# Batch-1 loads and statistics moved, and two layernorms without GpSimd, in a four-layer kernel built around a selective scan

## The chip, the cores and the metric

One core of one Trainium2 chip runs the whole program as a single launch. The metric is the device time of that launch in microseconds. The engines are named as in the profile: PE is TensorE (matrix products and transposes), DVE is VectorE, ACT is ScalarE, POOL is GpSimd, SP is SyncE, which here only issues DMAs.

## The reference

`x` is (2, 512, 512) in float32. Four residual sub-layers follow one another:

```
x = x + ln(scan_layer(ln(x)))     # selective scan, 1024 channels, 16 states
x = x + ln(ffn_4bit(ln(x)))       # 512 -> 1376 -> 512, 4-bit weights, output rounded to float16
x = x + ln(attention(ln(x)))      # 32 query heads, one key and value head
x = x + ln(experts(ln(x)))        # shared expert, latent expert, scaled by top-2 logits

def scan_layer(h):                # h is (2, 512, 512)
    x, gate = split(h @ W_in.T)                       # 1024 channels each
    x = silu(conv_b + causal_conv4(x))
    ts, Bm, Cm = split(x @ W_x.T, [32, 16, 16])       # the "ranks"
    ts, Bm, Cm = rms(ts), rms(Bm), rms(Cm)
    dt = softplus(ts @ W_dt.T + b_dt)
    for t in range(512):
        state = state * exp(dt[t] * A) + (dt[t] * x[t]) * Bm[t]   # 1024 x 16
        y[t] = sum over the 16 states of state * Cm[t]
    y = (y + x * D) * silu(gate)
    return y @ W_out.T

def ln(x): return (x - mean(x)) / sqrt(var(x) + 1e-5)  # the last one also has a scale and a shift
```

The 4-bit weights are `q * s - (z + 1) * s` in groups of 128 rows. The feed-forward layer computes `(g * sigmoid(g) * u) @ Wd` with `g = h @ Wg` and `u = h @ Wu`.

## The kernel before

The rows of `x` are eight tiles of 128 x 512, four to a batch; `xs(b)` gives those of batch b. Within the scan layer the data is transposed: 128 channels on the partitions and 512 time steps along the row. The 1024 channels are eight blocks c, so two batches make 16 blocks k = 8b + c. The 16 states are handled two at a time, in eight groups gi. A "scan step" s is one pair (k, gi): there are 128.

**Phase 1, the head** (to about 64 us). Batch 0 is normalized, projected and convolved, the ranks of batch 0 are computed, and 4-bit words of the gate and up weights are unpacked and stored to DRAM (`wgu_d`). `ranks_norm` and `ranks_out` scale the ranks and store B and C to DRAM (`scr`), from which `states(b, gi, "B")` loads each pair of rows to all partitions. At the end SP issues the 16 B and C loads (B of group gi + 1 ahead of C of group gi), and then, by `issue_after(last.ins)`, the four loads of batch 1's `x`. The statistics of batch 1 need these.

**Phase 2, the scan phase** (to about 584 us). One scan step is spread over the engines:

- ACT: `exps(s + 2)`, the decay exp(dt A) into one of two PSUM tiles `da`.
- DVE: `times_B` (L1055), `bx = du * B` with `du` in PSUM, then `scan` (L1059), the recurrence along the row in place in `bx`.
- POOL: `times_C` (L1065), and for some steps an addition of the two states (L1067).
- PE: `sums` (L1087), which adds the states up in the PSUM tile `py` with an identity matrix. `ps_y` has one buffer, so the sums of block k + 1 begin after `fin(k)` (L1093), where DVE multiplies the sum by the gate.

`bx` has six buffers. Beside its sums PE works through a generator, `stream()`: the gates of batch 0, batch 1's normalized and transposed x (`turned("n1")`), its projections and ranks, the gates of batch 1, the output projection of batch 0 (`out_tiles`), the transposes of the next sub-layer's input (`turned("f0")`), and the gate and up projections of feed-forward 0 for batch 0 (`ffn0`, L984). The loop gives it a budget: a step is worth `STEP = 3.5` us and a matmul costs `MM = 0.86`. What the other engines do with a result is a job: a generator that `spawn(gen, lag)` enters and that `tick()` advances, two ticks to a scan step. The order in which this loop emits instructions is the order in which each engine executes them: `pin()` fixes it. Two PSUM banks serve the stream (`bank`, `release`). `pool_turn()` lets one such job a step use POOL.

Three parts of this phase matter here:

- `norm_job(1, "n1")` computes the mean and variance of batch 1's four x tiles on DVE (L798, L799), and normalizes them. It is spawned with a lag of 12 ticks.
- `ranks_norm(1)` and `ranks_out(1)` do for batch 1 what the head did for batch 0. L513 and L514 turn the sums of squares into means, and L542 copies B and C out of PSUM.
- `out_job(i, ps)` takes the output projection of tile i of batch 0, normalizes it (`add_normed`: statistics on DVE, the power -1/2 and the product with the mean on POOL, the scaling on ACT, the residual addition L892 on POOL), and then normalizes the sum for feed-forward 0 (`norm_one`). `st["f0", i]` is the tick from which `turned("f0")` may transpose it.

**Phase 3** (from about 584 us). PE does the output projection of batch 1 (L1176). Meanwhile `once(dq)` unpacks the 4-bit down weights into DRAM (`wd_d`): `zeros` on DVE after the last `fin`, a store and a load of the zeros `z_d` (SP), eight words on DVE (L326) and POOL (L327), and stores. The second projection of feed-forward 0 (`fo`, L1198) reads them back. Feed-forward for batch 1, attention and the experts follow.

`w4` tiles (weights on the SP queue) and the output weights `wo` share a pool of three buffers, so a load waits in SP's order until a buffer has been read.

Of the kernel before, what the change touches and what calls it, by code (L numbers as in the profile page):

```python
# [9 lines left out]
F32 = mybir.dt.float32  # L10
# [8 lines left out]
P = 128  # L19
# [37 lines left out]
def tile_sandwich(  # L57
# [50 lines left out]

    def w4(src, name, chunks=KH, cols=PW):
        t_ = wst.tile([P, KH, PW], F32, tag="w4", name=name)  # L110
        nc.sync.dma_start(out=t_[:, :chunks, :cols], in_=src)
        return t_
# [17 lines left out]
    def minus_mean(mv, rs, name, n=TB, beside_scan=False):  # L130
# [12 lines left out]
        return nm  # L143

# [281 lines left out]
    with ExitStack() as mamba:  # L426
# [75 lines left out]
        def ranks_norm(b, ps):  # L502
# [10 lines left out]
            nc.vector.tensor_scalar(r[:, :, 0], ss[:, :, 0], 1.0 / R_DT, 1e-6, ALU.mult, ALU.add)  # L513
            nc.vector.tensor_scalar(r[:, :, 1:], ss[:, :, 1:], 1.0 / N_ST, 1e-6, ALU.mult, ALU.add)  # L514
# [24 lines left out]
        def ranks_out(b, pt):  # L539
            bc = st["bc"] = jrow(f"bc{b}")  # L540
            nc.scalar.copy(dtT[b][:R_DT, :], pt[:R_DT])
            nc.vector.tensor_copy(bc[R_B:N_ROW], pt[R_B:N_ROW])  # L542
# [30 lines left out]
        with ExitStack() as p1:  # L573
# [76 lines left out]
            half_gate = mbank("pg0_1")  # L650
            for k in range(KH // 2):
                nc.tensor.matmul(
                    half_gate, w_in(1, 0, 0)[:, k, P : 2 * P], xT[0][:, k, :], start=(k == 0), stop=False
                )
            for _ in ranks_norm(0, pr):
                pass
            ranks_out(0, ranks_rows(0, bank1(0, "pt0")))

            for gi in range(NGI):
                if gi + 1 < NGI:  # L660
                    states(0, gi + 1, "B")
                states(0, gi, "C")
# [3 lines left out]
            with tc.issue_after(last.ins):  # L666
                load_x(1)
# [7 lines left out]
        with ExitStack() as p2:  # L675
# [75 lines left out]
            def gate(b, c):  # L751
# [3 lines left out]
                if (b, c) == (0, 1):  # L755
                    turns.append([f"pg{b}_{c}", None])
                    ps = half_gate
                    yield from in_proj(b, ps, w, c % 2, KH // 2)
# [34 lines left out]
            def norm_job(b, name):  # L793

                mv = stat.tile([P, TB, 2], F32, tag="mv", name=f"mv_{name}")
                for i, src in enumerate(xs(b)):
                    s6 = stat.tile([P, 6], F32, tag="st", name=f"st_{name}_{i}")
                    nc.vector.bn_stats(s6, src)  # L798
                    nc.vector.bn_aggr(mv[:, i, :], s6)  # L799
                    yield 1  # L800
                yield 1
                rs = rstd(mv, name)
                nm = minus_mean(mv, rs, name, TB, True)
# [10 lines left out]
            def turned(name, dst):  # L814

                for i in range(TB):
                    yield from until((name, i), 2)
# [11 lines left out]
                    spawn(out(), 2)  # L829
# [38 lines left out]
            def norm_one(b, i, name):  # L868

                mv = moments([xs(b)[i]], f"{name}_{i}")  # L870
                rs = rstd(mv, f"{name}_{i}", 1)
                nm = minus_mean(mv, rs, f"{name}_{i}", 1, True)
                yield 4
# [6 lines left out]
                st[name, i, "xn"] = xn  # L880

# [19 lines left out]

            def out_job(i, ps):
                o = jrow(f"o0_{i}")
                if i < TB - 1:
# [575 lines left out]
```

## Time and profile before

| | |
|---|---|
| median of 3 runs | 957.5 us (957.22 to 958.73) |
| the profiled execution | 955.66 us, of which the span is 953.7 us |
| mean granted PE clock | 0.965 |
| scan phase, scan 0_0 to the last sum | about 64 to 578 us |
| one scan step on DVE | 1.20 (L1055) + 2.28 (L1059) us, less an overlap |
| batch 1's x: the four loads issued | from 81.90 us |
| first and last statistics of batch 1 (L798, L799) | 91.53 to 100.35 us |
| output projection of batch 1 | from 583.31 us |
| second projection of feed-forward 0 | from 612.77 us |

The profile page was taken on one execution. Its slices cut the span into 40 parts of 23.8 us, and each digit is a busy share in tenths. A row of the timeline gives the start and the duration in us, the engine, the line, the operation, what it writes and reads, the shape, and in brackets the idle time before it with what ended it. Line numbers in the prediction are those of the kernel before.

### The profile page before, as it was taken

The page shows a single profiled execution, that of the slowest core. Times are in us where ns is not written, and L with a number is a line of the kernel's source. Part 1 is how long each engine was busy: PE and PEld are TensorE (multiplying, and loading weights), DVE is VectorE, ACT ScalarE, POOL GpSimd, SP SyncE. Part 2 cuts the span into 40 slices and gives each one's busy share as a digit, 9 for nine tenths or more (in the row PEclk, how much of TensorE's full clock was granted, in tenths as well). Part 3 has the DMA queues.
Part 4 walks back from the last instruction along what each step waited for, and adds up shares of the span by engine and source line. Part 5 has one row for each costly group of instructions (what it writes and reads, how often), then busy time and mean ns, then how long its engine had stood idle before and what let it go on. Part 6 is the DMA issues. An engine that isn't in the chain of part 4 may idle for free.

```text
span 953.7 us, 7163 instructions
## 1 busy us (share of the span) xinstructions
PE 860.8 (90%) x2188; PEld 385.4 (40%) x2188; DVE 672.4 (71%) x780; ACT 424.1 (44%) x638; POOL 486.8 (51%) x356
## 2 busy tenths in 40 slices
PE   6989778789999889589999999999999998999994
PEld 3433333334533434134434444444544444455441
DVE  5877999999999998999999995535600024525225
ACT  4356675656666655476655640125320013412122
POOL 7746796677877787876877884440000000011002
PEclk9989999888999999889999999999999999999998
DMA  6449111010002854200111103445222231100101
GB/s 201 156 141 376 52 37 38 30 37 30 22 23 91 293 194 142 89 0 0 45 44 45 30 9 125 153 156 198 57 65 74 60 101 44 67 12 23 56 0 44
DMA packets 43816, 80.08 MB, mean 84 GB/s; under 512 B 7774, under 2 KB 20937, under 8 KB 43778
## 3 DMA queue, kind: packets, MB, share of 16 engines
q1 hardware_dynamic: 41506, 73.64, 23.4%
q0 software_dynamic: 1984, 5.47, 1.6%
q10 hardware_dynamic: 288, 0.52, 0.1%
q8 instruction: 17, 0.28, 0.1%
q14 instruction: 21, 0.17, 0.1%
HBM read 68.37 MB, written 11.24 MB: 83 GB/s over the span
## 4 chain that ended last, share of the span: by engine, by line
PE 48%; DVE 24%; issue 9%; POOL 7%; DMA 3%; ACT 2%; SPq 0%; DVEq 0%; POOLq 0%; ACTq 0%
DVE bx L1059 10%; DVE bx L1055 6%; PE py L1087 6%; PE pd L1408 6%; POOL bx L1065 5%; PE pup L1345 5%; PE fo L1198 4%; PE fg L371 4%; PE fu L371 4%; PE fo L1261 3%; PE fu L984 3%; PE fg L984 3%; PE po L1176 3%; PE po L953 2%; DVE u L483 2%
## 5 line engine op out<-in xcount | busy, mean ns | idle before, releaser
L1065 POOL TENSOR_TENSOR bx<-bx,C 128x1024 f32<-128x1024 f32 x128 | 301.8, 2358 | 117.4 <-DVE bx L1059 94.2
L1059 DVE TENSOR_TENSOR_SCAN bx<-da,bx 128x1024 f32<-128x1024 f32 x128 | 291.4, 2277 | 0.1
L1087 PE MATMUL py<-bx,ident 128*128 128x512 f32 x480 | 234.9, 620 | 41.4 <-POOL bx L1065 36.3
L1039 ACT ACTIVATE da<-dt,A 128x511 f32<-128x511 f32 x256 | 176.6, 691 | 170.1 <-DVE bx L1059 163.4
L1087 PEld LDWEIGHTS py<-bx,ident 128*128 128x128 f32 x480 | 90.8, 197 | 168.1 <-issue 91.7
L1055 DVE TENSOR_TENSOR bx<-du,B 128x1024 f32<-128x1024 f32 x127 | 152.8, 1203 | 5.7 <-DMA B<-scr 2.2
L1274 DVE TENSOR_TENSOR it<-it,fu 128x512 f32<-128x512 f32 (+1 forms) x11 | 7.5, 686 | 75.2 <-PE fu L371 75.2
L385 POOL TENSOR_TENSOR sd<-ve,half 128x4 f16<-128x4 f16 x2 | 2.1, 1042 | 110.7 <-DVE ve L383 110.7
L1345 PE MATMUL pup<-hT_l,wup 128*128 128x512 f32 x128 | 57.8, 606 | 0.0
L741 PE MATMUL pg<-xT,w_g 128*128 128x512 f32 x116 | 56.5, 619 | 0.0
L1408 PE MATMUL pd<-wdn,hid 128*128 128x512 f32 x128 | 55.3, 593 | 0.0
L127 POOL TENSOR_TENSOR rs_lo<-ve_lo,mhalf 128x1 f32<-128x1 f32 x8 | 5.4, 680 | 76.7 <-DVE ve_lo L125 76.7
L371 PE MATMUL fg<-hT_f,wg 128*128 128x512 f32 (+1 forms) x88 | 41.9, 614 | 0.7 <-ACT hT_f L171 0.7
L984 PE MATMUL fg<-hT_f,wg 128*128 128x512 f32 (+1 forms) x88 | 42.1, 597 | 0.0
L984 PE MATMUL fu<-hT_f,wu 128*128 128x512 f32 (+1 forms) x88 | 40.7, 592 | 0.0
L483 DVE SCALAR_TENSOR_TENSOR u<-px,ch,u 128x511 f32<-128x511 f32 (+2 forms) x48 | 35.8, 746 | 6.9 <-ACT u L476 5.8
L1261 PE MATMUL fo<-wd,it 128*128 128x512 f32 (+1 forms) x88 | 40.5, 603 | 0.0
L371 PE MATMUL fu<-hT_f,wu 128*128 128x512 f32 (+1 forms) x88 | 39.8, 593 | 0.0
L1198 PE MATMUL fo<-wd,it 128*128 128x512 f32 (+1 forms) x88 | 38.0, 594 | 1.8 <-DMA wd<-wd_d 1.8
L1408 PEld LDWEIGHTS pd<-wdn,hid 128*128 128x128 f32 x128 | 24.2, 190 | 30.7 <-issue 30.1
L1345 PEld LDWEIGHTS pup<-hT_l,wup 128*128 128x128 f32 x128 | 24.3, 193 | 28.8 <-issue 28.8
L1273 ACT ACTIVATE it<-fg 128x512 f32<-128x512 f32 (+1 forms) x11 | 6.6, 597 | 65.7 <-PE fg L371 65.7
(238 smaller groups left out, 1164.8 us busy)
## 6 DMA issues: line engine op xcount, KB each, us to landing
wo<-in_W_outT SPq DMA_DIRECT2D x20, 512.0 KB
B<-scr SPq DMA_DIRECT2D x16, 512.0 KB
C<-scr SPq DMA_DIRECT2D x16, 512.0 KB
wg<-wgu_d SPq DMA_DIRECT2D x10, 512.0 KB
wu<-wgu_d SPq DMA_DIRECT2D x10, 512.0 KB
w_x<-in_W_in SPq DMA_DIRECT2D x8, 512.0 KB
wgu_d<-w_gu POOLq DMA_DIRECT2D x16, 256.0 KB, 2.4
w_g<-in_W_in SPq DMA_DIRECT2D x8, 512.0 KB
```

Source lines behind the costliest of these rows:

```text
L371: nc.tensor.matmul(ps[:m], w[:, kc, e * P : e * P + m], hT[:, kc, :], start=(kc == 0), stop=(kc == KH - 1),)
L741: nc.tensor.matmul(ps, w[:, k, ts(e, P)], xT[b][:, k, :], start=(k == 0), stop=(k == KH - 1))
L984: nc.tensor.matmul(ps[:m], wt[j][a][:, kc, e * P : e * P + m], hT[:, kc, :], start=(kc == 0), stop=(kc == KH - 1),)
L1039: nc.scalar.activation(das[s % 2][:, i, 1:], st["dt", b, c][:, 1:], AF.Exp, scale=A[:, c, n : n + 1])
L1055: nc.vector.tensor_mul(bx, st["du"].unsqueeze(1).to_broadcast([P, NG, S]), Bbs[b][gi])
L1059: nc.vector.tensor_tensor_scan(flat, das[s % 2].rearrange("p n t -> p (n t)"), flat, 0.0, ALU.mult, ALU.add)
L1065: nc.gpsimd.tensor_mul(bxs[s], bxs[s], Cbs[b][s % NGI])
L1087: nc.tensor.matmul(st["y"], ident, bx[:, i, :], start=False, stop=last)
L1198: nc.tensor.matmul(fo[t], its[i][:m, ts(t, P)], w[:m, e], start=(i == 0), stop=(i == len(IC) - 1),)
L1261: nc.tensor.matmul(fo[t], its[i][:m, ts(t, P)], w[:m], start=(i == 0), stop=(i == len(IC) - 1),)
L1345: nc.tensor.matmul(ps, w[:, kc, ts(e, P)], src[kc], start=(kc == 0), stop=(kc == KH - 1))
L1408: nc.tensor.matmul(pd, hid[kc][:, ts(i, P)], wdn[kc], start=(kc == 0), stop=(kc == INT // P - 1),)
```

## The change

Five things are changed.

1. The loads of batch 1's x stand in SP's order after the first gate weights' load, the last one that `w4` had issued by then. In the order of the B and C loads each B moves up one place and each C down one. The first part of the gate of block 1 takes three of four slices of the contraction ahead of the ranks, where it took two.
2. `norm_job` computes the sums on ACT, with `accum_out`: the negative mean, and then the sum of squared deviations. The variance's scaling, the power and the product run on POOL. It is spawned with a lag of 2.
3. For batch 1, L513 and L514 run on POOL and the copy of L542 on ACT.
4. The last two tiles of batch 0 (i = 2, 3) go through `late_tile`: the statistics come from PSUM, the reciprocal root from an integer estimate and four Newton steps on DVE (`rstd_newton`, 16 operations of 128 x 1 with the mean's product), the residual addition is done on DVE, and the second norm follows at once.
5. The transposes of these two tiles wait one tick rather than two, and so does the copy of each.

```diff
@@ -106,9 +106,11 @@
     wgt = const.tile([P, KH, NE], F32, name="wgt")
+    issued = []
     def w4(src, name, chunks=KH, cols=PW):
         t_ = wst.tile([P, KH, PW], F32, tag="w4", name=name)
-        nc.sync.dma_start(out=t_[:, :chunks, :cols], in_=src)
+        issued.append(nc.sync.dma_start(out=t_[:, :chunks, :cols], in_=src))
         return t_
     def moments(srcs, name):
@@ -141,6 +143,21 @@
             nm[:, :n], mv[:, :n, 0], -1.0, rs[:, :n], ALU.mult, ALU.mult
         )
         return nm
+    def rstd_newton(mv, name):
+        v = stat.tile([P, 1], F32, tag="nv", name=f"nv_{name}", bufs=2)
+        nc.vector.tensor_scalar(v, mv[:, 0, 1:2], 1e-5, None, ALU.add)
+        yi = stat.tile([P, 1], I32, tag="ny", name=f"ny_{name}", bufs=2)
+        nc.vector.tensor_scalar(yi, v.bitcast(I32), 1, None, ALU.logical_shift_right)
+        nc.vector.tensor_scalar(yi, yi, -1.0, float(0x5F3759DF), ALU.mult, ALU.add)
+        y = yi.bitcast(F32)
+        t = stat.tile([P, 1], F32, tag="nt", name=f"nt_{name}", bufs=2)
+        for _ in range(4):
+            nc.vector.scalar_tensor_tensor(t, y, v[:, 0:1], y, ALU.mult, ALU.mult)
+            nc.vector.tensor_scalar(t, t, -0.5, 1.5, ALU.mult, ALU.add)
+            nc.vector.tensor_mul(y, y, t)
+        return y
     def scale_bias(mv, name, n=TB):
         rs = rstd(mv, name, n)
@@ -510,8 +527,9 @@
             )
             nc.vector.tensor_reduce(ss[:, :, 1:], sq[:, :, R_DT // N_ST :], AX.X, ALU.add)
             r = stat.tile([P, TB, 3], F32, tag="rr", name=f"rr{b}")
-            nc.vector.tensor_scalar(r[:, :, 0], ss[:, :, 0], 1.0 / R_DT, 1e-6, ALU.mult, ALU.add)
-            nc.vector.tensor_scalar(r[:, :, 1:], ss[:, :, 1:], 1.0 / N_ST, 1e-6, ALU.mult, ALU.add)
+            eng = nc.gpsimd if b else nc.vector
+            eng.tensor_scalar(r[:, :, 0], ss[:, :, 0], 1.0 / R_DT, 1e-6, ALU.mult, ALU.add)
+            eng.tensor_scalar(r[:, :, 1:], ss[:, :, 1:], 1.0 / N_ST, 1e-6, ALU.mult, ALU.add)
             yield 1
             if b:
                 nc.gpsimd.tensor_tensor(r, r, mhalf3, ALU.pow)
@@ -539,7 +557,10 @@
         def ranks_out(b, pt):
             bc = st["bc"] = jrow(f"bc{b}")
             nc.scalar.copy(dtT[b][:R_DT, :], pt[:R_DT])
-            nc.vector.tensor_copy(bc[R_B:N_ROW], pt[R_B:N_ROW])
+            if b:
+                nc.scalar.copy(bc[R_B:N_ROW], pt[R_B:N_ROW])
+            else:
+                nc.vector.tensor_copy(bc[R_B:N_ROW], pt[R_B:N_ROW])
             sc = dram.tile([N_ROW - R_B, S], F32, tag=f"scr{b}", name=f"scr{b}")
             nc.sync.dma_start(out=sc, in_=bc[R_B:N_ROW])
             scr.append(sc)
@@ -647,11 +668,13 @@
             root = stat.tile([P, 1], F32, tag="root", name="root", bufs=1)
             nc.scalar.activation(root, half[:, 0:1], AF.Sqrt)
-            half_gate = mbank("pg0_1")
-            for k in range(KH // 2):
+            first_gate = mbank("pg0_1")
+            for k in range(KH - 1):
                 nc.tensor.matmul(
-                    half_gate, w_in(1, 0, 0)[:, k, P : 2 * P], xT[0][:, k, :], start=(k == 0), stop=False
+                    first_gate, w_in(1, 0, 0)[:, k, P : 2 * P], xT[0][:, k, :], start=(k == 0), stop=False
                 )
+            with tc.issue_after(issued[-1].ins):
+                load_x(1)
             for _ in ranks_norm(0, pr):
                 pass
             ranks_out(0, ranks_rows(0, bank1(0, "pt0")))
@@ -659,12 +682,12 @@
             for gi in range(NGI):
                 if gi + 1 < NGI:
                     states(0, gi + 1, "B")
-                states(0, gi, "C")
+                if gi:
+                    states(0, gi - 1, "C")
+            states(0, NGI - 1, "C")
             last = states(0, 0, "B")
             gw.word()
             dt_out(0, 0, dt_in(0, 0, bank1(0, "pv0_0")))
-            with tc.issue_after(last.ins):
-                load_x(1)
             pin()
         g1p = pool(mamba, "mg1", 1)
@@ -754,8 +777,8 @@
                     w_in(1, b, c + 2 - c % 2)
                 if (b, c) == (0, 1):
                     turns.append([f"pg{b}_{c}", None])
-                    ps = half_gate
-                    yield from in_proj(b, ps, w, c % 2, KH // 2)
+                    ps = first_gate
+                    yield from in_proj(b, ps, w, c % 2, KH - 1)
                 else:
                     ps = yield from bank(f"pg{b}_{c}")
                     yield from in_proj(b, ps, w, c % 2)
@@ -794,13 +817,23 @@
                 mv = stat.tile([P, TB, 2], F32, tag="mv", name=f"mv_{name}")
                 for i, src in enumerate(xs(b)):
-                    s6 = stat.tile([P, 6], F32, tag="st", name=f"st_{name}_{i}")
-                    nc.vector.bn_stats(s6, src)
-                    nc.vector.bn_aggr(mv[:, i, :], s6)
-                    yield 1
-                yield 1
-                rs = rstd(mv, name)
-                nm = minus_mean(mv, rs, name, TB, True)
+                    xn = jrow(f"xj_{name}_{i}")
+                    nc.scalar.activation(
+                        xn, src, AF.Identity, scale=-1.0 / H, accum_out=mv[:, i, 0:1]
+                    )
+                    yield 2
+                    nc.scalar.activation(
+                        xn, src, AF.Square, bias=mv[:, i, 0:1], accum_out=mv[:, i, 1:2]
+                    )
+                    yield 2
+                yield from pool_turn()
+                ve = stat.tile([P, TB], F32, tag="ve", name=f"ve_{name}")
+                nc.gpsimd.tensor_scalar(ve, mv[:, :, 1], 1.0 / H, 1e-5, ALU.mult, ALU.add)
+                rs = stat.tile([P, TB], F32, tag="rs", name=f"rs_{name}")
+                nc.gpsimd.tensor_tensor(rs, ve, mhalf, ALU.pow)
+                nm = stat.tile([P, TB], F32, tag="nm", name=f"nm_{name}")
+                nc.gpsimd.tensor_mul(nm, mv[:, :, 0], rs)
                 yield 3
                 for i in range(TB):
                     yield 2
@@ -814,7 +847,8 @@
             def turned(name, dst):
                 for i in range(TB):
-                    yield from until((name, i), 2)
+                    lag = 1 if name == "f0" and i >= TB - 2 else 2
+                    yield from until((name, i), lag)
                     tp = yield from bank(f"tp_{name}_{i}")
                     tp = tp.rearrange("p (k t) -> p k t", k=KH)
                     for kc in range(KH):
@@ -826,7 +860,7 @@
                         st[name, i, "free"] = st[name, "out"] = now[0]
                         yield 1
-                    spawn(out(), 2)
+                    spawn(out(), lag)
                     yield MM / 2
                 for i in range(TB):
                     while (name, i, "free") not in st:
@@ -865,12 +899,7 @@
                 spawn(out(), 2)
                 yield MM / 2
-            def norm_one(b, i, name):
-                mv = moments([xs(b)[i]], f"{name}_{i}")
-                rs = rstd(mv, f"{name}_{i}", 1)
-                nm = minus_mean(mv, rs, f"{name}_{i}", 1, True)
-                yield 4
+            def spread_out(b, i, name, rs, nm):
                 xn = jrow(f"xn_{name}_{i}")
                 apply(
                     xn.rearrange("p (k a r) -> p r k a", k=KH, a=2),
@@ -878,6 +907,14 @@
                 )
                 st[name, i] = now[0]
                 st[name, i, "xn"] = xn
+            def norm_one(b, i, name):
+                mv = moments([xs(b)[i]], f"{name}_{i}")
+                rs = rstd(mv, f"{name}_{i}", 1)
+                nm = minus_mean(mv, rs, f"{name}_{i}", 1, True)
+                yield 4
+                spread_out(b, i, name, rs, nm)
             def add_normed(b, i, src, o):
@@ -899,16 +936,32 @@
                 nc.sync.dma_start(out=w, in_=w_out[j])
                 return w
+            def late_tile(i, ps, o):
+                mv = moments([ps], f"mo0_{i}")
+                rs = rstd_newton(mv, f"mo0_{i}")
+                nm = minus_mean(mv, rs, f"mo0_{i}", 1)
+                yield 1
+                apply(o, ps, rs, nm, 0)
+                release(f"po0_{i}")
+                yield 2
+                nc.vector.tensor_add(xs(0)[i], xs(0)[i], o)
+                mv = moments([xs(0)[i]], f"f0_{i}")
+                rs = rstd_newton(mv, f"f0_{i}")
+                nm = minus_mean(mv, rs, f"f0_{i}", 1)
+                yield 1
+                spread_out(0, i, "f0", rs, nm)
             def out_job(i, ps):
                 o = jrow(f"o0_{i}")
-                if i < TB - 1:
+                if i < TB - 2:
                     nc.scalar.copy(o, ps)
                     release(f"po0_{i}")
                     yield 3
                     yield from add_normed(0, i, o, o)
                 else:
-                    yield from add_normed(0, i, ps, o)
-                    release(f"po0_{i}")
+                    yield from late_tile(i, ps, o)
+                    return
                 yield 1
                 yield from norm_one(0, i, "f0")
@@ -1100,7 +1153,7 @@
             pe = stream()
             spawn(words_job(), 4)
-            spawn(norm_job(1, "n1"), 12)
+            spawn(norm_job(1, "n1"), 2)
             d0 = jrow("d0")
             nc.vector.tensor_mul(d0, u[0][0], st["dt", 0, 0])
```

## The prediction

> **What bounds the kernel now.** I read the engine totals, the slices, busy time by stage, VectorE's waits between 64 and 584 us (the scan phase), and the timeline at each place that the diff touches.
>
> ```profile
> span 953.7 us, 7163 instructions
> PE 860.8 (90%) x2188; PEld 385.4 (40%) x2188; DVE 672.4 (71%) x780; ACT 424.1 (44%) x638; POOL 486.8 (51%) x356
> DVE  5877999999999998999999995535600024525225
> PEclk9989999888999999889999999999999999999998
> ```
>
> TensorE is busiest overall, but that is an average of two halves: VectorE is full in slices 5 to 24, TensorE after them. By stage (columns: PE, weight loads, DVE, ACT, POOL, clock, DMA share, GB/s):
>
> ```profile
> 110.00:330.00 220.00, 192.98 (x485) 85.24 (x484) 214.86 (x162) 143.81 (x220) 168.45 (x94) 0.95 0.18 59
> 480.00:530.00 50.00, 48.52 (x110) 19.96 (x109) 49.93 (x35) 31.82 (x48) 41.71 (x22) 1.00 0.15 42
> ```
>
> VectorE works 214.86 of 220 us and 49.93 of 50. Until the last scan ends at 572.1 us, a microsecond added to or taken from VectorE's queue, work or wait, moves the end of the scans by one. Its waits that the change touches:
>
> ```profile
> DVE st_n L798 <- DMA x<-in_x_in: 3.5, 1, 3.5
> DVE bc L542 <- ACT dtT L541: 2.8, 1, 2.8
> DVE bx L1055 <- DMA B<-scr: 2.2, 1, 2.2
> DVE st_f L119 <- POOL x L892: 1.9, 2, 1.5
> ```
>
> What follows the scans:
>
> ```profile
> 578.37 0.69 DVE L1093 TENSOR_TENSOR g<-g,py 128x512 f32<-128x512 f32 x1 [3.67 <-PE py L1087]
> ...
> 583.31 27.63 PE L1176 MATMUL po<-wo,g 128*128 128x512 f32 x64
> 583.51 0.38 SPq L899 DMA_DIRECT2D wo<-in_W_outT  x1
> 584.26 0.61 SPq L227 DMA_DIRECT2D z_d<-zd_d  x1
> 587.84 1.29 DVE L326 TENSOR_TENSOR w_d<-q_d,z_d 128x512 f32<-128x512 int32 x2 [3.57 <-DMA z_d<-zd_d]
> ```
> ```profile
> 612.77 3.70 PE L1198 MATMUL fo<-wd,it 128*128 128x512 f32 x8 [1.82 <-DMA wd<-wd_d]
> ```
>
> The last scan's sum lets fin run at 578.37. TensorE then still does the last gate and up of feed-forward 0 (578.2 to 583.3), the output projection of batch 1 (27.6 us), and waits 1.82 us for dequantized down weights. These hang on fin by another road: fin, zeros, store, the load of z_d at 584.26, w_d from 587.84, and fo 24.9 us later. After that TensorE has hardly a gap, so the end moves with fo's start.
>
> **Part by part, VectorE in the scan phase (minus is gain).**
>
> Head. SP now issues the four x loads about 20 us before their old place (81.90), ahead of two gate-weight loads, the store of the ranks and all B and C loads. These 1 MB fall into TensorE-bound time before the ranks are stored; I cost that at 0 (cover: the store is issued at 63.29; uncovered, at most about the old x landing, 3 us). B2 comes one queue place sooner: its wait of 2.17 ends with a landing at 73.56, and the place ahead landed at 72.25: −1.3. C comes a place later; POOL waits, and six bx buffers stand between that and VectorE: 0. The wait for x: −3.45. The four statistics (.69 + .18, net .85 each): −3.4. In their place ACT gets 8 activations of .65 to .85 us (5 to 7 us) between 66 and 100, where it idles some 10; some land ahead of an exp that a scan needs, +.6. Sum −7.5.
>
> Batch-1 ranks. The copy at 286.89 goes to ACT with its 2.84 wait: −3.5. The two rr operations (1.14 and .16) go to POOL: −1.1. ACT and POOL are not full here. All gains: −12.1.
>
> The two late tiles: four norms, each with a 16-instruction chain for one ve. The nearest row for a dependent 128x1 operation:
>
> ```profile
> 384.13 0.18 DVE L120 BATCH_NORM_AGGREGATE mv_f<-st_f 128x2 f32<-128x6 f32 x1
> 384.35 0.15 DVE L125 TENSOR_SCALAR ve_f<-mv_f 128x1 f32<-128x1 f32 x1
> 384.42 0.14 DVE L125 TENSOR_SCALAR ve_mo<-mv_mo 128x1 f32<-128x1 f32 x1
> ```
>
> ve_f starts .04 after its input ends and lasts .15; the independent ve_mo comes .07 later. So .19 to .2 per dependent step, .07 if steps could overlap. I take .195, as each step reads the one before: 15 × .195 × 4 = +11.7 (bounds 4.2 and 13). Two residual additions come from POOL (1.26 there), about .6 each: +1.2. The statistics' wait on POOL's x goes (1.48 and .45): −1.9.
>
> Locks. The scan and the B product take one input from PSUM. Of the 16 chain steps 8 read two SBUF tiles, and so does the addition.
>
> ```profile
> 591.65 0.68 DVE L326 TENSOR_TENSOR w_d<-q_d,z_d 128x512 f32<-128x512 int32 x1
> 592.40 1.39 POOL L327 TENSOR_TENSOR w_d<-w_d,s_d 128x512 f32<-128x512 f32 x1 [0.96 <-DVE w_d L326]
> 592.70 1.64 DVE L326 TENSOR_TENSOR w_d<-q_d,z_d 128x512 f32<-128x512 int32 x1
> ```
>
> The same two-SBUF subtraction takes .68 alone and 1.64 when it meets POOL's product, ending .55 after that. By contrast the one-input ve_mo took .14 at 356.69 with POOL's C product under way. The Trainium skill ("SBUF — State Buffer", Who interferes with whom) says that a VectorE instruction with two SBUF inputs contends with a GpSimd instruction that reads SBUF, and the later one is fully blocked. It speaks against this change: POOL is busy three quarters of the time here, in pieces of 2.35 and 1.27. By the ve row alone locks cost 0 and the phase ends even; by the rule a chain can wait for one POOL piece and each addition for part of one. Laying the new order of both queues side by side gives f_2 2.1, f_3 .9, others .1 to .4: I take +3.2 (bounds 0 and 7).
>
> Sum of the late tiles: 11.7 + 1.2 − 1.9 + 3.2 = +14.2. One gate-up product that ran after the scans now runs before scan 7_5: +.6. Scan 7_5 (ended 566.5) moves by −12.1 + 14.2 + .6 = +2.7.
>
> **From there to the end.** The tiles leave POOL (.55 + .26 per norm, 1.26 per addition), so the transposes of f_2, f_3 and the first gate come about five scan steps earlier on TensorE. The first gate is no sooner than py_2, whose start waits for fin g_1 since ps_y has one buffer. Still, all of feed-forward 0 ends before the last sum, and TensorE does not have 5 us of it left. The last product now stands before scan 7_7 and waits about 1.7 there for POOL, but POOL's gate product (1.27 at 572.71) is out of the last C products' way: fin comes 11.5 after scan 7_5 instead of 11.87, at about +2.3.
>
> The output projection starts as fin ends, near 581 instead of 583.31. TensorE waits for the down weights all the same. That road gets shorter: SP stood at a wo load until 583.51 for TensorE's up products, and z_d lands 3.58 after its issue behind 512 KB of wo. Without both, z_d comes 2.8 sooner after fin. fo: +2.3 − 2.8 = −.5. The dequantization is what is late next: TensorE's gap before fo grows from 1.8 to about 4 us.
>
> A gap has a price here:
>
> ```profile
> 337.54 2.90 PE L953 MATMUL po<-wo,g 128*128 128x512 f32 x3 [3.30 <-DMA wo<-in_W_outT]
> ```
>
> Three matmuls after a 3.30 us wait took 2.90 us against 1.85 at L1087's mean of .62: +1. The skill ("TensorE: Matmul & The Clock Gate", Part 1) says an idle window of 3.4 us halves the clock until 3.4 us of work have passed: with that the price is up to 1.7. I take the row, +1. Total −.5 + 1 = +.5: the profiled execution goes from 955.66 (1.96 beside its span of 953.7) to 956.2. It lies 1.84 below the median 957.5, so the forecast is 958.0.
>
> **The rivals.** What this kernel's measurement can tell from no change is about .2%, 1.9 us (its three runs spread over 1.5).
> 1. Near even, as summed: 958.0, own range 955.6 to 960.4. Chance .46.
> 2. Slower: locks. VectorE's two-input steps meet POOL again and again, because POOL still has a backlog of C products when a chain starts and slips one in whenever a one-input step runs. Place: the four chains, between scans 1_3 and 2_2. Price: two POOL pieces per chain and one per addition, about 7 to 9 in all instead of 3.2, so +4 to +6: 962 to 964. It decides from 5 us of lock waits on. For: POOL's load and the row of 1.64. Against: POOL's next C product needs a scan that is queued behind the chain, so its backlog is one or two pieces. Chance .26.
> 3. Faster: the chain is cheap. At .1 us a step it costs 6 instead of 11.7, and locks shrink with it: scan 7_5 at −3 to −4, fo likewise: 952 to 954. For: .07 between independent steps. Against: every step depends on the last. The same end if dequantization follows fin by more than 2.8 less. Chance .26.
> 4. The change does not do what it says: feed-forward 0 still trails because ps_y or the banks hold it. TensorE's 5 us come back, the end follows fin: 959 to 960. Chance .02.
>
> Faster by over .2%: case 3 and the lower edge of 1, .30. Within: .32. Slower: case 2 and the upper edge, .38. Range 952 to 964.5.
>
> **What would show it.** Right: scan 1_0 (105.67) at about 98; no L542 on DVE near 284; chain steps of .15 each .19 apart; a two-input step or addition of over 1 us beside a POOL product; f_2's gate about 17 us earlier; no L984 after fin; L1176 at 581; fo at 612 after a wait of 4. Wrong: chain steps below .12 or above .25 apart; ACT's statistics making scans wait over 1.5 us; fo starting with no wait, or at a time that does not follow fin by about 32.

## The result: half a percent slower

| | before | after |
|---|---|---|
| median of 6 runs | 958.24 us (957.22 to 960.64) | 963.43 us (962.70 to 966.44) |
| ratio to before, 95% interval | | 1.0058 (1.0037 to 1.0079) |
| the profiled execution, its span | 955.66, 953.7 | 966.44, 964.7 |

The median moved by 5.2 us, the two profiled executions by 10.8. The one of before lies 2.6 below its median and the one of after 3.0 above. So positions inside the traces are compared below, and how much of them is in the medians is said where it matters.

The page of the changed kernel, the lines that answer to those shown of before:

```profile
span 964.7 us, 7220 instructions
PE 871.3 (90%) x2188; PEld 390.3 (40%) x2188; DVE 683.0 (71%) x830; ACT 428.8 (44%) x654; POOL 482.7 (50%) x348
DVE  5878999999999989999999995525510024525225
PEclk9989999889999998689999999999999999999998
```

VectorE has 50 instructions and 10.6 us more. The 6 in the clock row (385.9 to 410.0 us) is the place of the late tiles: TensorE is busy for less than half of it, since its inputs come behind VectorE's chains, and its clock falls to .6. VectorE's waits:

```profile
DVE du L1106 <- ACT du L1100: 3.9, 2, 2.1
...
DVE it L1025 <- POOL it L742: 1.8, 1, 1.8
...
DVE bx L1108 <- DMA B<-scr: 0.4, 1, 0.4
```

The wait for batch 1's x is gone, as is the copy's (2.84) and most of the second B's. A wait of 3.9 us in two pieces, for `du`, was not among the prediction's. Where the scans stand, after against before (minus is earlier), gives a ledger:

| start of | before | after | shift | predicted |
|---|---|---|---|---|
| scan of batch 0, block 1, group 0 (scan 1_0) | 105.67 | 100.11 | −5.56 | −7.5 |
| batch 1, block 0, group 7, ahead of the late tiles | 356.75 | 347.56 | −9.19 | −12.1 |
| batch 1, block 2, group 4, behind them | 414.42 | 420.12 | +5.70 | +2.1 |
| batch 1, block 7, group 5 (scan 7_5) | 564.32 | 570.52 | +6.20 | +2.7 |
| the last scan | 569.83 | 578.49 | +8.66 | |
| fin | 578.37 | 585.92 | +7.55 | +2.3 |
| first w_d | 587.84 | 592.43 | +4.59 | −.5 |
| fo | 612.77 | 618.13 | +5.36 | −.5 |

**The waits that were handed on.** ScalarE, VectorE and ScalarE again, at the two places of the wait for `du`:

```profile
91.31 0.60 ACT L737 ACTIVATE th<-pg 128x512 f32<-128x512 f32 x1 [2.35 <-PE pg L764]
...
94.15 0.57 ACT L1100 COPY du<-dt 128x512 f32<-128x512 f32 x1
```
```profile
94.76 0.70 DVE L1106 TENSOR_TENSOR du<-u,du 128x512 f32<-128x512 f32 x1 [1.85 <-ACT du L1100]
```
```profile
279.20 0.58 ACT L561 COPY bc<-pt 32x512 f32<-32x512 f32 x1
...
283.83 0.60 ACT L737 ACTIVATE th<-pg 128x512 f32<-128x512 f32 x1 [2.74 <-PE pg L764]
...
286.67 0.57 ACT L1100 COPY du<-dt 128x512 f32<-128x512 f32 x1
```

ScalarE stands at a gate that TensorE has not finished, then does the gate and an exp, and only then the copy that VectorE's next block starts from. In the trace of before ScalarE also waited for that gate (1.87 at 90.28), while VectorE was waiting for x.

**The late tiles.** The second norm of tile 2, on VectorE and on GpSimd:

```profile
376.45 1.17 DVE L948 TENSOR_TENSOR x<-x,o 128x512 f32<-128x512 f32 x1
...
378.98 0.15 DVE L153 TENSOR_SCALAR ny_f<-ny_f 128x1 int32<-128x1 int32 x1
379.16 1.89 DVE L157 SCALAR_TENSOR_TENSOR nt_f<-ny_f,nv_f 128x1 f32<-128x1 f32 x1
381.09 0.15 DVE L158 TENSOR_SCALAR nt_f<-nt_f 128x1 f32<-128x1 f32 x1
381.28 0.16 DVE L159 TENSOR_TENSOR ny_f<-ny_f,nt_f 128x1 f32<-128x1 f32 x1
381.48 0.22 DVE L157 SCALAR_TENSOR_TENSOR nt_f<-ny_f,nv_f 128x1 f32<-128x1 f32 x1
```
```profile
375.81 1.26 POOL L1120 TENSOR_TENSOR bx<-bx 128x512 f32<-128x512 f32 x1
377.03 1.71 POOL L929 TENSOR_TENSOR x<-x,o 128x512 f32<-128x512 f32 x1
378.70 2.34 POOL L1118 TENSOR_TENSOR bx<-bx,C 128x1024 f32<-128x1024 f32 x1
```

The first two-tile step takes 1.89 instead of .22: it ends at 381.05, GpSimd's product at 381.04. Every later step is clean, since GpSimd's next product needs a scan that stands behind the chain. The addition meets GpSimd's pair addition, which ends at 377.07, and ends .55 behind it, as the subtraction at 592.70 did in the trace of before. It takes 1.17; two SBUF tiles of this shape take .69 alone (d from u and dt at 65.39). GpSimd's own next addition (L929) is held up in its turn: 1.71 instead of 1.26.

**The tail**, VectorE, GpSimd and TensorE:

```profile
577.89 0.68 DVE L1025 TENSOR_TENSOR it<-it,fu 96x512 f32<-96x512 f32 x1 [1.78 <-POOL it L742]
578.49 2.28 DVE L1112 TENSOR_TENSOR_SCAN bx<-da,bx 128x1024 f32<-128x1024 f32 x1
```
```profile
580.92 2.34 POOL L1118 TENSOR_TENSOR bx<-bx,C 128x1024 f32<-128x1024 f32 x1 [0.75 <-DVE bx L1112]
```
```profile
618.13 12.26 PE L1251 MATMUL fo<-wd,it 128*128 128x512 f32 x24 [3.71 <-DMA wd<-wd_d]
```

The last gate-up product stands ahead of the last scan, and GpSimd's last C product waits for that scan. Feed-forward 0 no longer trails, and fo follows after a wait of 3.71.

### The profile page after: what moved, and what is told of

Read it like the earlier page. It is cut to its first block, busy times and chain, and to the rows that moved or that the text cites. A ratio compares the mean times of both kernels' runs of the same rounds, so it can differ in the third digit from the quotient of the medians.

```text
span 964.7 us, 7220 instructions
## 1 busy us (share of the span) xinstructions
PE 871.3 (90%) x2188; PEld 390.3 (40%) x2188; DVE 683.0 (71%) x830; ACT 428.8 (44%) x654; POOL 482.7 (50%) x348
## 4 chain that ended last, share of the span: by engine, by line
PE 38%; DVE 31%; issue 13%; POOL 6%; ACT 4%; DMA 2%; SPq 1%; DVEq 0%; POOLq 0%; ACTq 0%
DVE bx L1112 11%; DVE bx L1108 9%; PE pd L1461 6%; PE pup L1398 5%; PE py L1140 4%; PE fu L388 4%; PE fg L388 4%; PE fo L1314 3%; PE po L1006 2%; DVE u L500 2%; POOL bx L1118 2%; PE fo L1251 2%; PE pr L1429 1%; PE pg L764 1%; POOL w_d L344 1%
## 5 line engine op out<-in xcount | busy, mean ns | idle before, releaser
L1140 PE MATMUL py<-bx,ident 128*128 128x512 f32 x480 | 239.3, 628 | 29.4 <-POOL bx L1118 21.4
L1140 PEld LDWEIGHTS py<-bx,ident 128*128 128x128 f32 x480 | 93.1, 200 | 156.9 <-issue 98.8
L388 PE MATMUL fu<-hT_f,wu 128*128 128x512 f32 (+1 forms) x88 | 42.4, 624 | 0.0
L1037 PE MATMUL fu<-hT_f,wu 128*128 128x512 f32 (+1 forms) x88 | 40.4, 594 | 1.4 <-ACT dt L588 1.4
```

Source lines behind the costliest of these rows:

```text
L388: nc.tensor.matmul(ps[:m], w[:, kc, e * P : e * P + m], hT[:, kc, :], start=(kc == 0), stop=(kc == KH - 1),)
L1037: nc.tensor.matmul(ps[:m], wt[j][a][:, kc, e * P : e * P + m], hT[:, kc, :], start=(kc == 0), stop=(kc == KH - 1),)
L1140: nc.tensor.matmul(st["y"], ident, bx[:, i, :], start=False, stop=last)
```

## The experiments

The theory after this ledger (V): up to the last scan every microsecond in VectorE's queue moves the scans by one, so the late tiles cost what they put on VectorE. The rival (P): TensorE, full from 440 us on, sets the pace there. All ratios are to runs of the kernel before made beside these.

**e1: without the late tiles.** The head and ranks as changed.

```diff
-                    lag = 1 if name == "f0" and i >= TB - 2 else 2
+                    lag = 2
...
-                if i < TB - 2:
+                if i < TB - 1:
...
-                    yield from late_tile(i, ps, o)
-                    return
+                    yield from add_normed(0, i, ps, o)
+                    release(f"po0_{i}")
```

> The changed kernel with the last two tiles of batch 0 as in the kernel before (no late_tile, lags of 2); the head, the batch-1 statistics and the ranks as changed. Theory V (VectorE's ledger): the 9.1 us that the scans were ahead at scan 1_1_2 in the changed kernel are kept to the last scan, since nothing after it differs from the kernel before; fo and the end follow, 957.5 - 9.1 = about 948.5. Rival P (TensorE binds from 440 us on, where it was busy 40.0 of 40 and 48.5 of 50 us, so scans that are ahead wait for sums and banks): a third to all of the lead is lost before the last scan, 952 to 958.

Measured: 949.14 us, ratio .9914 (.9897 to .9930). The scan of batch 1, block 2, group 4 starts 8.10 earlier than before, the one of block 7, group 5 8.10 earlier (556.22), fin 8.10 (570.27), fo 8.16 (604.61). The lead passes undiminished through the 130 us from 440 on, in which TensorE is full. P is out: TensorE's order there is tied to the scans, and it starts earlier with them. fin waits as it did before (3.67 there):

```profile
570.27 0.69 DVE L1146 TENSOR_TENSOR g<-g,py 128x512 f32<-128x512 f32 x1 [3.66 <-PE py L1140]
```

The lead was 8.1 and not 9.1 because this run's head gave less (3.92 at scan 1_0 for 5.56): VectorE waited 2.83 for the second B, which it did not in the changed kernel, and 2.75 instead of 1.85 for `du`.

**e2: the late tiles alone, with their short lags, on the kernel before.**

```diff
+    def rstd_newton(mv, name):
...
+            def late_tile(i, ps, o):
...
-                if i < TB - 1:
+                if i < TB - 2:
...
-                    yield from add_normed(0, i, ps, o)
-                    release(f"po0_{i}")
+                    yield from late_tile(i, ps, o)
+                    return
```

> The kernel before with the late tiles alone (late_tile, Newton steps on VectorE, lags of 1). Theory V: the scans from scan 1_1_2 to 1_2_4 fall behind by 14.9 us as in the changed kernel, about 1.4 more until fin, 3 us come back in the dequantization of the down weights: 957.5 + 14 = about 971. Rival P: the earlier transposes and gates of feed-forward 0 relieve TensorE, and a good part of the 14.9 is recovered before the last scan: 960 to 966.

Measured: 973.75 us, ratio 1.0169 (1.0149 to 1.0189). Across the late tiles the scans fall from +1.06 to +15.94, that is 14.88, the 14.89 of the changed kernel. fin comes at 596.35 (+18.0), fo at 627.96 (+15.2): 2.8 us come back, in dequantization, and nothing before it. V holds; this half of the change alone costs 1.7%. The long steps came again as in the changed kernel: 1.90 and .68 at the first two-tile steps, 1.17 and 1.16 at the additions.

**e3: two Newton steps for four.**

```diff
-        for _ in range(4):
+        for _ in range(2):
             nc.vector.scalar_tensor_tensor(t, y, v[:, 0:1], y, ALU.mult, ALU.mult)
```

> The changed kernel with two Newton steps in place of four (the reciprocal root is then good to about 5e-6 by estimate). One step took .63 us in the changed kernel's trace, so VectorE has 2 x .63 x 4 = 5.0 us less in the four norms. Theory V: all of it reaches the end: 963.4 - 5.0 = 958.4. Rival P (TensorE sets the pace after the norms): less than half does, 961 to 963.4. Locks as the cost, rather than the steps: the wait of about 1.7 at f_2's first two-input step stays, and the gain is still 5.

Measured: 956.92 us, ratio .9996 (.9981 to 1.0011), a gain of 6.5 us in the medians on the changed kernel. Across the late tiles VectorE loses 9.79 instead of 14.89, which is 5.1 less, and the first two-tile step keeps its wait (1.90). So the steps pay in full. Scan 7_5 starts 4.79 before that of the changed kernel (this run's head was 1.1 behind) and fo, at 612.50, 5.63 before.

**e4: the power on GpSimd, the rest of the late tiles kept.**

```diff
-                rs = rstd_newton(mv, f"mo0_{i}")
-                nm = minus_mean(mv, rs, f"mo0_{i}", 1)
+                rs = rstd(mv, f"mo0_{i}", 1)
+                nm = minus_mean(mv, rs, f"mo0_{i}", 1, True)
```

(and the same for `f0`)

> The changed kernel with the power -1/2 and the mean's product of the two late tiles on GpSimd again, everything else of late_tile (statistics from PSUM, residual addition on VectorE, lags) kept. VectorE loses 15 steps of .19 in each of four norms (11.4 us) and the lock waits inside the chains (about 2). Theory V: 963.4 - 13 plus what VectorE's additions now wait for GpSimd's power and ScalarE's scaling (0 to 2 each): 950.5 to 955. Rival W (the wait that the Newton chain was put there to remove is as long as the chain): the additions and the exps behind the scaling wait 5 us and more each, 960 or above.

Measured: 950.08 us, ratio .9917 (.9901 to .9933). From the scan ahead of the late tiles to the one behind them VectorE loses .38 us, where it lost 14.89 with the chain. It pays 1.17 and 1.16 for the additions, and neither waits:

```profile
374.66 1.17 DVE L948 TENSOR_TENSOR x<-x,o 128x512 f32<-128x512 f32 x1
...
392.96 1.16 DVE L948 TENSOR_TENSOR x<-x,o 128x512 f32<-128x512 f32 x1
```

ScalarE stands for GpSimd's results ahead of the second scaling, but in this stretch the exps behind it are not late for a scan:

```profile
380.18 1.29 ACT L167 ACTIVATE xn_f<-x,nm_f,rs_f 128x512 f32<-128x512 f32 x1 [2.78 <-POOL nm_f L136]
...
397.24 1.26 ACT L167 ACTIVATE xn_f<-x,nm_f,rs_f 128x512 f32<-128x512 f32 x1 [2.74 <-POOL nm_f L136]
```

So the chain took away a wait that VectorE does not feel, and W is out. A little later, at group 7 of that block, VectorE waits for a `du` (.84) and for the first gate-up product (1.44). At scan 7_5 the lead over before is 5.65, where e1 has 8.10; in fo e4 is back to within .8 of e1.

**g1: the chain with one tile per step.**

```diff
-            nc.vector.scalar_tensor_tensor(t, y, v[:, 0:1], y, ALU.mult, ALU.mult)
+            nc.vector.tensor_scalar(t, y, y[:, 0:1], v[:, 0:1], ALU.mult, ALU.mult)
...
-            nc.vector.tensor_mul(y, y, t)
+            nc.vector.tensor_scalar(y, y, t[:, 0:1], None, ALU.mult)
```

> The changed kernel with the two-tile steps of the Newton chain written with one tile and per-partition scalars instead (y * y * v and y * t as tensor_scalar); the same number of steps and the same result. Theory L (the two-input steps are held up by GpSimd's reads): the waits of 1.67 and .46 us at the first step of f_2 and f_3 go, and the 16 scalar_tensor_tensor steps of .22 become .15 to .18: 963.4 - 3 = about 960.5; the additions keep their 1.17. Rival S (per-partition scalars are read over the same interface, or the long first step had another cause): the long steps stay, 962.5 to 963.4.

Measured: 962.58 us, ratio 1.0054 (1.0033 to 1.0075). The long steps are gone, as theory L has it:

```profile
380.70 0.15 DVE L153 TENSOR_SCALAR ny_f<-ny_f 128x1 int32<-128x1 int32 x1
380.89 0.27 DVE L157 TENSOR_SCALAR nt_f<-ny_f,nv_f 128x1 f32<-128x1 f32 x1
381.20 0.15 DVE L158 TENSOR_SCALAR nt_f<-nt_f 128x1 f32<-128x1 f32 x1
381.39 0.21 DVE L159 TENSOR_SCALAR ny_f<-ny_f,nt_f 128x1 f32<-128x1 f32 x1
```

But the steps got longer, not shorter: .27 and .21 for .22 and .16. That is .1 for each of 16 Newton iterations, 1.6 against the 2.1 that the locks had cost. From the scan ahead of the late tiles to the one behind them VectorE lost 14.51 instead of 14.89. So the steps are held up by their second tile, as L says, but the gain that L forecast (3 us) did not come: the time, 962.58, lies in the range of the rival S.

**f1: VectorE's product without ScalarE's copy, for two blocks, on e1.**

```diff
-                nc.scalar.copy(du, st["dt", b, c])
+                if k not in (1, 7):
+                    nc.scalar.copy(du, st["dt", b, c])
...
-                    nc.vector.tensor_mul(st["du"], u[b][c], st["du"])
+                    nc.vector.tensor_mul(st["du"], u[b][c], st["dt", b, c] if k in (1, 7) else st["du"])
```

> The run without late tiles (949.1), with ScalarE's copy of dt into the PSUM tile du left out for blocks 1 and 7: VectorE's product u * dt reads dt from SBUF there, so it waits for nothing on ScalarE. Theory Q (VectorE waits at the first du because ScalarE's queue stands at a gate that TensorE has not finished): the two waits of 4.8 us in that run's trace go, less up to 1.7 each if the two-SBUF product meets a C product of GpSimd: 949.1 - 4.8 + 1 = about 945. Rival N (TensorE itself is behind at these two places, and VectorE's next need of it, a sum or a free buffer, comes as late): the waits turn up a few steps later, 948 to 949.5.

Measured: 946.73 us, ratio .9879 (.9864 to .9894), the fastest of all. Both waits for `du` are gone, and the product took .68 and 1.07. The scan of block 0, group 7 is 4.3 us ahead of e1, 1.4 of it from ahead of the product. But new waits stand in the list of this run:

```profile
DVE bx L1109 <- issue: 2.5, 1, 2.5
DVE u L500 <- ACT u L493: 2.5, 2, 2.2
```

The second is for the most part one at 141.65 (2.17), where ScalarE had itself waited 3.15 for TensorE's `px`; the first stands at 338.76, and the trace does not show what ended it. At scan 7_5 the lead over e1 is .75 us, and fo starts at 604.87 against 604.61. So for the scans the rival N holds: the lead is lost again at later needs. The 2.4 us that the median gained lie behind fo (340.7 us from fo to the end in this trace, 344.2 in that of e1), where the edit changes no instruction. In these two traces the 3.5 us are TensorE's clock (below, at g2). Why the median keeps 2.4 of them stays open.

**f2: the copy of B and C on VectorE, on e1.**

```diff
-            if b:
-                nc.scalar.copy(bc[R_B:N_ROW], pt[R_B:N_ROW])
-            else:
-                nc.vector.tensor_copy(bc[R_B:N_ROW], pt[R_B:N_ROW])
+            nc.vector.tensor_copy(bc[R_B:N_ROW], pt[R_B:N_ROW])
```

> The run without late tiles (949.1), with the copy of batch 1's B and C back on VectorE. Theory H (the wait was partly handed on: 2.84 at the copy became 2.1 at the du of block 7): VectorE loses 2.84 + .66 = 3.5 at the copy and gets 2.1 back at that du: 949.1 + 1.4 = 950.5. Rival I (the du wait has nothing to do with the copy): it stays, 952.6.

Measured: 951.65 us, but spread from 947.06 to 953.72 (ratio .9920, .9900 to .9941), which tells 1.4 from 3.5 poorly. The trace does it: at the copy (scan of block 6, group 4) the lead over before falls from 9.66 in e1 to 6.20, by 3.46, and at block 6, group 7, where e1 loses 2.19 to its wait for `du`, f2 loses nothing. That leaves 1.27, as theory H has it: the wait was partly handed on. Of the 3.5 us that moving the copy gains at the copy, 2.2 are given back at the next block. Further on, at batch 1's block 0, group 5, the two runs part by another .75, beside a wait of 2.0 in f2 whose cause the trace does not show; at scan 7_5 f2 is 2.05 behind e1.

**f3: late tiles with power and addition on GpSimd, and du as in f1.**

```diff
-                nc.vector.tensor_add(xs(0)[i], xs(0)[i], o)
+                nc.gpsimd.tensor_add(xs(0)[i], xs(0)[i], o)
+                yield 1
```

> Late tiles without the Newton chain and without VectorE's addition: statistics from PSUM on VectorE, power, mean's product and residual addition on GpSimd, the short lags kept, and du as in the run f1. Theory V: against the run with the power on GpSimd (950.1) VectorE has two additions of 1.16 less, but waits for GpSimd's x up to 1.9 as in the kernel before, and the du waits go (-4): 945 to 947. Against f1 it has the earlier feed-forward 0, worth 1.7 us between scan 7_5 and fo: the two should be within 2 us. Rival P (feed-forward 0 earlier is what pays): 941 to 943.

Measured: 950.96 us (946.77 to 954.76), ratio .9923 (.9900 to .9946). Worse than expected: the statistics wait for GpSimd's sum longer than the additions had cost VectorE.

```profile
DVE st_f L121 <- POOL x L948: 5.4, 2, 3.0
```

So with these short lags the addition is cheaper on VectorE (2 x 1.16). And feed-forward 0 that starts earlier pays little: fo follows scan 7_5 by 47.3 us here, 46.7 in e4 and 48.4 in e1.

**f4 and g2: TensorE's gap ahead of fo filled** with seven and with three extra matmuls, on the changed kernel.

```diff
+            for n in range(7):
+                nc.tensor.matmul(fo[n % 2], its[0][:, 0:P], its[n][:, 0:H], start=True, stop=True)
```

(in g2 `range(3)`)

> The changed kernel with seven extra matmuls (results overwritten) in TensorE's gap of 3.7 us ahead of the second projection of feed-forward 0. Theory G (the gap costs clock: the first ten matmuls after it took 6.26 us against 4.6 at full clock): fo starts at the same time and its first ten take 4.6, -1.5: about 962. Rival Z (the slower start is only where the run's clock happened to fall): no change, 963.4, and a slow stretch elsewhere.

> The changed kernel with three extra matmuls (results overwritten; two passes of .45 us each, 2.7 us) in TensorE's gap of 3.7 us ahead of the second projection of feed-forward 0; the order of every queue is otherwise that of the changed kernel, which the run with seven was not. Theory G (the gap costs clock): fo starts at the same time, and its first ten us hold 24 passes at clock 1.00 instead of 20 at .83: 963.4 - 1.8 = 961.6. Rival Z: the first ten us stay at 20 to 21 passes, 963.4.

f4 measured 969.37 us, ratio 1.0119 (1.0102 to 1.0136), and answers another question than it was made for. Each float32 matmul stands in the trace as two passes of about .45, so seven took some 6.2 us, more than the gap. And SP's order changed: two more loads of attention weights than in the changed kernel came ahead of a down-weight load, for which TensorE then waited:

```profile
644.54 19.11 PE L1253 MATMUL fo<-wd,it 128*128 128x512 f32 x40 [4.20 <-DMA wd<-wd_d]
```

g2 measured 961.72 us, ratio 1.0046 (1.0029 to 1.0062). TensorE's first ten microseconds of fo, in the changed kernel, in g2, in e1 and in e2 (columns: the stretch, its length, PE busy with its passes, the granted clock, DMA share, GB/s):

```profile
618.13:628.13 10.00, 10.00 (x20) 0.83 0.32 111
```
```profile
616.45:626.45 10.00, 10.00 (x24) 1.00 0.35 120
```
```profile
604.61:614.61 10.00, 10.00 (x24) 1.00 0.39 133
```
```profile
627.96:637.96 10.00, 10.00 (x24) 1.00 0.35 121
```

Theory G is right on the place: with the gap of 3.71 left open 20 passes fit, with it filled or with e1's 1.77 there are 24. Four passes are 1.7 us. That this is the 1.7 by which g2's median is lower is not shown: the intervals of the two ratios overlap, g2's fo came 1.68 earlier in its trace, and its remainder from fo to the end (345.7) is hardly shorter than the changed kernel's (346.6).

But the length of the gap does not decide. e2's gap of 3.12 cost nothing, while those of e4 (2.83), f3 (3.02), g1 (3.04) and e3 (3.15) were followed by .83 like the changed kernel's. The traces show what does. From 60 us on, in all twelve of them, the granted clock changes only at instants that are whole multiples of 3.41 us apart, and it is either full or half. Where this grid lies differs from run to run. Here are the stretches of the grid around the gap in the changed kernel, in g1 and in e2:

```profile
615.26:618.67 3.41, 0.54 (x2) 1.00 0.86 323
618.67:622.09 3.42, 3.42 (x6) 0.50 0.53 175
```
```profile
616.70:620.11 3.41, 1.35 (x3) 1.00 0.96 345
620.11:623.52 3.41, 3.41 (x5) 0.50 0.48 169
```
```profile
622.97:626.38 3.41, 1.88 (x5) 1.00 0.27 72
626.38:629.79 3.41, 1.83 (x5) 1.00 0.82 309
629.79:633.21 3.42, 3.42 (x9) 1.00 0.50 168
```

In the changed kernel TensorE idled for 2.87 us of one stretch, in g1 for 2.06, and the next stretch ran at half clock. e2's longer gap fell across two stretches, with 1.53 and 1.58 idle, and neither was followed by a drop. At this place all twelve runs agree: 2.06 or more idle in a stretch brought a drop, 1.86 or less did not. (The profile models the ends of matmuls, so these lengths are not exact.) One drop costs half of 3.41, 1.71 us.

This also accounts for what lies behind fo. From there to the last matmul the trace of before has four drops and that of the changed kernel seven; TensorE's idle time is the same (20.4 and 20.7 us). Three drops are 5.1 of the 5.6 us by which the remainders differ. f1 has four and e1 six, 3.4 of their 3.5 us. Not every drop follows a gap: the changed kernel's at 680.11 comes behind a stretch in which TensorE was busy throughout, with matmuls of 48 columns. What brings those was not tested.

## Why the prediction came out as it did

The range (952 to 964.5) holds 963.43. The forecast of 958.0, no change, was 5.4 too low, and its own range (955.6 to 960.4) does not hold the result. The number is that of the second rival, but not for its reason, so that it lies within the wide range is luck.

1. **Bound and ledger: right.** The end follows VectorE's queue up to the last scan. e1, e2 and e3 show it from both sides.
2. **Gains, 12.1: mis-sized, 9.2.** The step that failed is "ACT and POOL are not full here": it took ScalarE's idle time as a sign that work moved there would cost VectorE almost nothing. The work was rightly taken off VectorE: the x wait, the statistics, the two rr operations and the copy went. The second B's wait (2.17) went too, one us more than forecast, but the next three scans gave that back, .36 for a B and .30 for an exp among it. What was missed is order. ScalarE takes its instructions in the order of the program, VectorE needs its copy to `du` once a block, and at both places that copy stood behind a gate that TensorE had not finished. The two waits for `du`, 1.85 and 2.06, are 3.9 us. f1 removes both, and VectorE waits later instead, the first time behind TensorE's px; so TensorE is what is late next, and ScalarE need not be full for that. The question that was not put is the prediction's own: once a wait is gone, what is late next? The x loads were issued at 32.11, 50 us before their old place and not 20. That they cost the head nothing held: its first scan starts at 68.62, before at 68.04, and between 67.42 and 68.62 in the ten runs with this head.
3. **Late tiles, +14.2: right, 14.9.** The steps start .19 after one another as taken, but .25 after the two-tile scalar_tensor_tensor (.22 long), so the chains cost about .8 more in all. Locks: +3.2 forecast; 1.67 and .46 at first steps and .48 and .46 at the additions (1.17 and 1.15 against .69) make 3.1. They fell where they were forecast, 2.15 on f_2 (2.1) and .92 on f_3 (.9). Here the row of the two-SBUF subtraction and the Trainium skill's rule ("SBUF — State Buffer", Who interferes with whom) decided rightly against the row of ve_mo: by that row alone the tiles would have cost 11, and g1, which takes the second tile out of the steps, removes the two long ones.
4. **Rival 2, locks at 7 to 9: wrong.** The reason against it held: GpSimd's next product needs a scan behind the chain, so each chain met one product at most. **Rival 3, cheap chain at .1 a step: wrong.** **Rival 4, feed-forward 0 still trails: wrong**, it ended ahead of fin.
5. **fin, 11.5 after scan 7_5's end: wrong.** Forecast was .4 less than before, measured 1.35 more. The wait of the last gate-up product ahead of scan 7_7 was sized well (1.78), but it was taken that GpSimd's C products set the end. The last one waits .75 for the scan.
6. **Dequantization, −2.8: right.** fin to the first w_d is 6.51 instead of 9.47. But w_d to fo is 25.70 instead of 24.93, +.8 that the prediction carried over unchanged.
7. **Clock after the gap, +1: right in kind.** The trace shows 1.7, in four passes. The skill's rule ("TensorE: Matmul & The Clock Gate", Part 1), an idle window of about 3.4 us, put it by estimate at up to 1.7. The size is as measured, and a grid of 3.41 us is in the traces. But a stretch of it need not be idle throughout: 2.06 of 3.41 us were enough (g1). Whether a gap of about 3 us costs anything was therefore chance from run to run (e2 against g1), and the forecast could not know it.

Summed: −9.2 + 14.9 + .5 at scan 7_5, +1.35 at fin, −2.96 and +.77 to fo, is 5.4; the medians differ by 5.2. Against the forecast for fo (−.5) that is 5.9 too late: 2.9 for the gains, .7 for the tiles, 1.7 for fin and .6 for the dequantization. The further 5.6 us of the two traces lie behind fo (346.6 against 340.9), 5.1 of them in three more clock drops. They belong to these two executions: 5.6 is also what the two lie off their medians together.

## What to carry to other kernels

When work leaves a full engine for an idle one, look at what that engine delivers next to the full one, and in which order: ScalarE's queue, which stood at TensorE's unfinished gates, handed back 3.9 us. Before replacing another engine's operation by a chain of small dependent ones on the engine that binds, show the wait that it removes. Here 16 steps of 128x1, .19 to .25 us apart, cost 3.2 us a norm, and the wait that they saved was ScalarE's, not VectorE's (e4). A change of several parts deserves a run for each part: −8.5 (e1) and +16.1 us (e2) stood behind +5.2 (their sum is 7.6; in the traces e1's head gave 1.4 us less than that of the changed kernel and e2's was 1.1 late), and the good part alone is .9% faster than the kernel before, 1.2% with f1's two products.

## What the runs showed of the hardware

- A VectorE instruction with two SBUF tiles of 128x1 was blocked beside GpSimd's product although it reads one element per partition: 1.89 us for a step of .22, until the product ended; 1.90 in e2 and e3. It also holds GpSimd up: beside the two additions on VectorE GpSimd's next operations took 1.71 and 2.79 instead of 1.26 and 2.36.
- Per-partition scalars cost time on VectorE even at one element: tensor_scalar with one scalar from SBUF took .21, with two .27, with immediates .15 (g1). They did not wait for GpSimd's product, which ran from 380.43 to 382.77.
- ScalarE's accumulating activation brings a second instruction of .18 to .19 us that reads the accumulator, so one statistic of 128x512 took .70 (Identity) to .80 us (Square) from its start.
- The granted clock was full or half, and changed on a grid of 3.41 us that lies differently in every execution. Ahead of fo, a stretch with 2.06 us or more of TensorE idle time was followed by a stretch at half clock (1.71 us lost), one with 1.86 or less was not. The same gap can cost 1.7 us in one execution and nothing in the next.
- The same order of queues gave a lead at the scan of block 1, group 0 between 3.9 us (e1, e4) and 6.2 us (g2). In e1 VectorE waited 2.83 for the second B, in e4 .67 for a B and 1.75 for an exp; both waited 2.75 for `du`, g2 1.85. A head that waits for a load to all partitions is not reproducible to a microsecond here.
